# A fused layernorm, attention and FP4 feed-forward kernel: the feed-forward's inner values are kept in a pair of PSUM banks through SiLU's product and the quantizer

## The chip, the cores and the metric

The kernel runs on one core of one Trainium2 chip. The metric is the device time of one execution in microseconds (us). The kernel before takes 1505.81 us, the median of three runs (1504.54 to 1507.39).

## The reference, cut to what matters

The input `x` has the shape 4 x 2048 x 256, float32. The reference is a chain of four residual steps. Each one adds to `x` a function of `_layernorm(x)`: first attention a, then a feed-forward (FFN), then attention b, then the same FFN with the same weights.

```
def fp4_quant_dequant(x):                      # blocks of 16 along the last dimension
    scale = max(|block|) / 6, at least 1e-12
    q = nearest of {0, .5, 1, 1.5, 2, 3, 4, 6} to |block / scale|, with its sign, times scale
def fp4_linear(x, w): return einsum(fp4_quant_dequant(x), fp4_quant_dequant(w))
def ffn(x, w_gate, w_up, w_down):              # 256 -> 704 -> 256
    h = silu(fp4_linear(x, w_gate)) * fp4_linear(x, w_up)
    return fp4_linear(h, w_down)
```

Attention a normalizes its queries and keys over the whole tensor, and its output reduces to the value projection times s/s, so it needs one first pass over all of `x` (a Gram matrix). Attention b mixes the four rows of the leading dimension for each of the 2048 positions, in 16 heads of 16.

## The kernel before, in words

**Tiling.** The 2048 positions are cut into 16 groups of 128. A group is 128 partitions by 4 rows by 256 columns, so each of the two FFNs has 4 tiles of 128 rows in each group: 16 groups x 2 x 4 = 128 FFN tiles in all. The function `first_pass` prepares the weights and the Gram matrix; `group(j)` records everything that is done for one group.

**An FFN tile** (`ffn_tile`) goes over all five engines. TensorE multiplies the turned, quantized input with the gate and up weights, in two halves of 352 columns; each half has a PSUM bank for gate and one for up (line 1443). ScalarE takes SiLU of the gate half (L1464), and VectorE multiplies it with the up half and writes the product `h` to SBUF (L1475). The quantizer `to_grid` then works on all 704 columns of `h`, in SBUF: VectorE takes the block maxima and their reciprocals (`to_scales`, L383 and L384) and scales the values (`over_scales`, L388), ScalarE takes magnitudes (`to_steps`, L394), and VectorE rounds in two passes (`to_sum` L401, `from_sum` L404). The last pass writes bf16 values into `qm`. A DMA turns these (`gT`), other DMAs spread the turned scales (`hqT`, L1299), GpSimd multiplies the two (L1510), and TensorE multiplies with the down weights (L1547). The layout of `h` has a 17th column in each block that holds a constant floor for the scale, so L383 reads 748 columns.

**Other stages.** `attention_a` (projection at L1173 with `wvz`), `attention_b` (L1173 with `wqkB`, `wvgB`, `woB`; VectorE products at L1654 and sums at L1661, L1780, L1783; GpSimd at L1762), `ffn_in` (normalization and quantizer of the FFN's input, 1024 columns in one go), and `turn`, which transposes on TensorE (L1150) and drains on ScalarE (L1157).

**The order of the work.** Nothing is ordered by loops. Every step is recorded with `plan.op(engine, us, rank, fn, reads, writes, port)`: its engine, a cost in us, and a rank. `Plan.order` then plays the steps through by those costs. Whenever an engine is free, it takes the ready step of lowest rank whose buffers are free, and the instructions are emitted in the order in which the steps start. The engines' queues keep that order on the chip; semaphores make them wait for what isn't ready. The ranks come from the table `BEGIN`, with one row for each group.

**Two resources in the plan.** A step with `port=True` on VectorE or GpSimd takes a lock that the other's steps must wait for: the plan never lets two such steps overlap. All three quantizer passes of an FFN tile have `port=True` in the kernel before. Buffers come from pools: four PSUM banks called `mm` for gate and up halves, four called `bank` for everything else, three `h`, three `qa`, two `qm`, two `gT`, three `hqT`.

The costs that the plan uses are lines like these; 0.86 us is its price of one quantizer pass over 704 columns:

```
    SYNC = 0.08
    AHEAD = {"DVE": 0.15, "POOL": 0.08}
...
                {"amax": 1.32, "pass": 0.86, "abs": 0.74, "n": FF},
```

Of the kernel before, what the change touches and what calls it, by code (L numbers as in the profile page):

```python
# [18 lines left out]
P = 128  # L19
D = 256  # L20
# [4 lines left out]
HF = FF // 2  # L25
FB = FF // BLK

# [11 lines left out]
def blocks(ap, n=BLK):  # L39
    return ap.rearrange("p (g e) -> p g e", e=n)  # L40
# [17 lines left out]
class Plan:  # L58
# [4 lines left out]
    SYNC = 0.08  # L63

    WINDOW = 3.4133
    AHEAD = {"DVE": 0.15, "POOL": 0.08}
# [47 lines left out]
    def order(self, seed):  # L114
# [58 lines left out]
        while left:  # L173
            moved = False
            for e, ready in waiting.items():
# [42 lines left out]
                heapq.heappush(done, (now + us + o["land"], i))  # L218
# [5 lines left out]
            times = [t for t in free_at.values() if t > now + 1e-9]  # L224
# [8 lines left out]
            while done and done[0][0] <= now + 1e-9:  # L233
                t, i = heapq.heappop(done)
                for b in ops[i]["bufs"]:
                    b.left -= 1
                    if not b.left:
                        pools[b.pool].append(b.ap)
# [11 lines left out]
def kernel(  # L250
# [43 lines left out]
    banks = [one([P, 512], f"bank{i}", ps) for i in range(8)]  # L294
# [121 lines left out]
    plan.pool("mm", banks[:4])  # L416
    plan.pool("bank", banks[4:])
# [4 lines left out]
    floored += tiles("h", 3, [P, FB, BLK + 1], fp)  # L422
# [3 lines left out]
    tiles("sil", 2, [P, HF], fp)  # L426
    tiles("qa", 3, [P, FF], fp)

    for t in tiles("qm", 2, [P, 6 * P], fp, BF16):
        nc.gpsimd.memset(t[:, FF:], 0.0)  # L430
    tiles("gT", 2, [P, 6, P], fp, BF16)
# [3 lines left out]
    for t in tiles("hqT", 3, [P, 6, P], fp):  # L435
        nc.gpsimd.memset(t[P // 2 :, 5, :], 0.0)
# [15 lines left out]
    def first_pass():  # L452
        op = plan.op
        GRAM = [plan.given("bank", 2) for _ in range(KC)]
        gram = [b.ap for b in GRAM]

# [97 lines left out]
        def normalized_products(n, j):  # L554
# [3 lines left out]
            for s in range(S):  # L558
                op(
                    "ACT",  # L560
                    0.6,
# [89 lines left out]
        for ns in together:  # L651
            for n in ns:
# [21 lines left out]
                for s in range(S):  # L674
                    op(
                        "DVE",
                        0.465,
# [13 lines left out]
            if n >= SOON:  # L691
                op("POOL", 4.4, at + 3.0, lambda cut=cut: roots_later(cut), seen, done)
            else:
                y, _, v = (norm_tiles["a"][:, cut, i, :] for i in range(2, 5))
                op("DVE", 0.8, at + 0.5, lambda cut=cut: variances(cut), seen, done)
                op(
                    "ACT",
                    0.25,
# [6 lines left out]
                op("DVE", 1.0, at - 30.0, lambda cut=cut: inverses(cut), (), done)  # L705
# [11 lines left out]
        def quantize(at, load, p, n):  # L717
# [7 lines left out]
            def sc(i):  # L725
# [13 lines left out]
                0.25,  # L739
# [1142 lines left out]
```

## Time and profile before

| | |
|---|---|
| median of three runs | 1505.81 us (1504.54 to 1507.39) |
| the profiled execution: its time, its span | 1509.01 us, 1507.2 us |
| mean granted TensorE clock | 0.992 |
| PE (TensorE) busy | 1448.9 us, 96% of the span, 5742 matmul instructions |
| DVE (VectorE) busy | 1385.5 us, 92% |
| ACT (ScalarE) busy | 797.0 us, 53% |
| POOL (GpSimd) busy | 759.0 us, 50% |
| chain of work that ended last | PE 54%, DVE 22%, issue 4%, ACT 2%, POOL 1%, DMA 1% |

The profile page is of one execution. A row of its list of groups names a line of the kernel, the engine, the operation, what is written and read with shapes, and the count; then the busy time of all, the mean time of one, and the idle time of the engine just before them with what ended it. One float32 matmul of the program stands in the trace as two instructions. Matmuls overlap: the time of one contains the way through the array, so a matmul's mean time is longer than the distance at which matmuls follow each other. The table of waits sums, for each engine and line, the time that the engine stood idle and what released it. The timeline gives start, length, engine, line and count of instructions that follow each other.

### The profile page before, as it was taken

How to read it: one execution, taken by the hardware profiler on the slowest of the kernel's cores; microseconds unless marked ns; L12 is line 12 of the kernel's file. 1: busy time of each engine (PE TensorE's matmuls, PEld its weight loads, DVE VectorE, ACT ScalarE, POOL GpSimd, SP SyncE). 2: the span in 40 equal slices, each digit the busy share in tenths (PEclk: the TensorE clock that was granted, in tenths of full speed). 3: DMA queues.
4: the chain of work that ended last, by engine and by line, in shares of the span. 5: the costliest groups of instructions: out<-in, count | busy, mean ns of one | idle time of the engine just before them, and what ended most of it. 6: DMA issues, size and time to landing. Idle time of an engine off the chain costs nothing.

```text
span 1507.2 us, 19903 instructions
## 1 busy us (share of the span) xinstructions
PE 1448.9 (96%) x5742; PEld 1003.4 (67%) x5742; DVE 1385.5 (92%) x2139; ACT 797.0 (53%) x1696; POOL 759.0 (50%) x787
## 2 busy tenths in 40 slices
PE   7989999999999999999999999999979999999999
PEld 7746566666767676666666666677657766766676
DVE  7789899999999989999889999999989999899996
ACT  6556656542656355555375665365446543554342
POOL 5343455454754364544454654455655454754532
PEclk9999999999999999999999999999999999999999
DMA  9303321234432333233323332232323333322541
GB/s 280 91 1 51 61 35 19 46 60 79 88 61 50 63 65 70 62 67 64 67 47 60 67 57 59 50 61 61 59 42 65 63 58 67 65 47 49 95 80 42
DMA packets 220989, 96.86 MB, mean 64 GB/s; under 512 B 108240, under 2 KB 220624, under 8 KB 220880
## 3 DMA queue, kind: packets, MB, share of 16 engines
q1 hardware_dynamic: 220880, 95.60, 32.3%
q8 instruction: 45, 0.74, 0.2%
q14 instruction: 64, 0.52, 0.1%
HBM read 18.09 MB, written 8.39 MB: 18 GB/s over the span
## 4 chain that ended last, share of the span: by engine, by line
PE 54%; DVE 22%; issue 4%; ACT 2%; POOL 1%; DMA 1%; POOLq 0%; SPq 0%; DVEq 0%; ACTq 0%
PE bank L1443 24%; PE bank L1547 14%; PE bank L1173 12%; PE bank L1150 2%; DVE qa L401 2%; DVE sh L383 2%; DVE qa L388 2%; DVE qm L404 2%; DVE h L1475 2%; DVE pp L1654 2%; DVE pp L1780 2%; DVE sc L1661 1%; DVE x L335 1%; DVE qax L404 1%; DVE qax L401 1%
## 5 line engine op out<-in xcount | busy, mean ns | idle before, releaser
L1443 PE MATMUL bank<-wguT,turned 128*128 128x352 f32 x2048 | 641.1, 462 | 11.5 <-DVE h L1475 8.9
L1443 PEld LDWEIGHTS bank<-wguT,turned 128*128 128x128 f32 x2048 | 382.4, 191 | 219.2 <-issue 16.2
L1547 PE MATMUL bank<-wdT,hqT 128*128 128x256 f32 x1536 | 350.9, 380 | 4.4 <-POOL hqT L1510 3.1
L1510 POOL TENSOR_TENSOR hqT<-hqT,gT 128x768 f32<-128x768 f32 x124 | 231.1, 1869 | 214.1 <-DMA gT<-qm 68.9
L1547 PEld LDWEIGHTS bank<-wdT,hqT 128*128 128x128 f32 x1536 | 289.8, 190 | 63.8 <-POOL hqT L1510 8.5
L1464 ACT ACTIVATE sil<-bank 128x352 f32<-128x352 f32 x256 | 114.6, 454 | 114.6 <-PE bank L1443 88.4
L394 ACT ACTIVATE qm<-qa 128x704 bf16<-128x704 f32 (+2 forms) x136 | 105.6, 779 | 89.1 <-DVE qa L388 82.8
L1762 POOL TENSOR_TENSOR pp<-vg,sc 128x1024 f32<-128x1024 f32 x64 | 134.4, 2114 | 33.2 <-DVE tok L1783 28.8
L1475 DVE TENSOR_TENSOR h<-sil,bank 128x352 f32<-128x352 f32 x256 | 127.8, 506 | 24.9 <-ACT sil L1464 11.8
L401 DVE SCALAR_TENSOR_TENSOR qa<-qm,qa 128x704 f32<-128x704 bf16 (+2 forms) x136 | 137.9, 1014 | 12.9 <-ACT qm L394 12.8
L1266 POOL TENSOR_TENSOR qax<-qax,sx 128x1024 f32<-128x1024 f32 x32 | 71.1, 2222 | 127.9 <-DVE qax L404 95.8
L388 DVE SCALAR_TENSOR_TENSOR qa<-sh,h 128x704 f32<-128x704 f32 x128 | 131.6, 1038 | 0.7
L404 DVE SCALAR_TENSOR_TENSOR qm<-qm,qa 128x704 bf16<-128x704 bf16 x124 | 128.5, 1037 | 2.4
L1157 ACT COPY turned<-bank 128x512 f32<-128x512 f32 x160 | 87.5, 585 | 69.9 <-PE bank L1150 69.7
L1173 PE MATMUL bank<-wqkB,turned 128*128 128x512 f32 x256 | 123.3, 605 | 0.1
L383 DVE TENSOR_REDUCE sh<-h 128x44 f32<-128x748 f32 x128 | 119.1, 930 | 3.8
L1173 PE MATMUL bank<-wvz,turned 128*128 128x512 f32 x256 | 118.2, 595 | 2.1 <-ACT wdT L850 0.8
L341 ACT ACTIVATE dev<-x,norms_f 128x256 f32<-128x256 f32 x128 | 64.9, 507 | 56.0 <-DVE x L335 53.9
L1654 DVE TENSOR_TENSOR pp<-qk 128x1024 f32<-128x1024 f32 x64 | 84.4, 1319 | 0.4
L1173 PEld LDWEIGHTS bank<-wvz,turned 128*128 128x128 f32 x256 | 46.5, 190 | 49.1 <-issue 38.8
L377 ACT ACTIVATE xn<-x,norms_f 128x256 f32<-128x256 f32 x128 | 67.9, 592 | 20.6 <-POOL norms_f L371 16.8
L1661 DVE TENSOR_REDUCE sc<-pp 128x64 f32<-128x1024 f32 x64 | 77.6, 1213 | 1.3
(194 smaller groups left out, 2047.2 us busy)
## 6 DMA issues: line engine op xcount, KB each, us to landing
hqT<-sT SPq DMA_DIRECT2D x620, 64.0 KB
x<-in_L_attn_a_x_dram SPq DMA_DIRECT2D x23, 512.0 KB
out_dram<-x SPq DMA_DIRECT2D x64, 128.0 KB
hqT<-sT SPq DMA_DIRECT2D x124, 32.0 KB
gT<-qm SPq DMA_TRANSPOSE x124
hqT<-in_L_ffn_w_down_dram SPq DMA_DIRECT2D x2, 352.0 KB
hqT<-in_L_ffn_w_gate_dram SPq DMA_DIRECT2D x5, 128.0 KB
hqT<-in_L_ffn_w_up_dram SPq DMA_DIRECT2D x5, 128.0 KB
```

The source lines that it names most:

```text
L383: nc.vector.tensor_reduce(amax, src, AX.X, ALU.max, apply_absolute_value=True)
L388: nc.vector.scalar_tensor_tensor(blocks(a), over_blocks(rs), -6.0 * BELOW, src, ALU.mult, ALU.mult)
L401: nc.vector.scalar_tensor_tensor(a, m, FLOOR, a, ALU.max, ALU.add)
L404: nc.vector.scalar_tensor_tensor(a if to is None else to, m, FLOOR, a, ALU.max, ALU.subtract)
L1173: nc.tensor.matmul(bank.ap[:, :n], lhs.ap[:, c, s * P : (s + 1) * P], w[:, c, :], start=(c == 0), stop=(c == KC - 1),)
L1443: nc.tensor.matmul(bank.ap[:, :HF], xqT.ap[:, c, s * P : (s + 1) * P], w[:, c, cols], start=(c == 0), stop=(c == KC - 1),)
L1464: lambda g=g, sil=sil: nc.scalar.activation(sil.ap, g.ap[:, :HF], AF.Silu),
L1475: lambda u=u, sil=sil, half=half: nc.vector.tensor_mul(h.ap[:, half * FB // 2 : (half + 1) * FB // 2, :BLK], blocks(sil.ap), blocks(u.ap[: ...
L1510: lambda: nc.gpsimd.tensor_mul(hqT.ap, hqT.ap, gT.ap),
L1547: nc.tensor.matmul(o.ap[:, :D], hqT.ap[:, i, :], wdT[:, i, :], start=(i == 0), stop=(i == 5),)
L1654: nc.vector.tensor_mul(pr.ap, qk.ap[:, s : s + 1, :D].to_broadcast([P, S, D]), qk.ap[:, :, D:],)
L1762: nc.gpsimd.tensor_mul(pv.ap.rearrange("p t (n e) -> p t n e", e=HD), vg.ap[:, :, :D].rearrange("p t (n e) -> p t n e", e=HD), over_blocks ...
```

## The change

- **FFN tile.** The 704 columns are cut into 512 and 192 in place of 352 and 352. The first 512 gate columns go to a bank. The 512 up columns go to the first bank of a pair of banks (`pair`, two pairs in all); the remaining 192 up columns and the remaining 192 gate columns go to the second bank of the same pair (the step `rest`). The product with SiLU is written over the up values in the pair, the block maxima go into the pair's free columns, and the quantizer's passes work in place in the pair. Only the last pass writes to SBUF (`qm`). `h` and its 17th column are gone; the floor of the scale is a small extra VectorE instruction. The three passes no longer carry `port=True`.
- **Buffers.** Eight single banks become two pairs and four single banks; the pool `mm` is gone, so the gate bank comes from `bank` as all other products do. `qm` goes from 2 to 4, `gT` from 2 to 3, `hqT` from 3 to 4, `qa` from 3 to 2.
- **Plan.** A step's result now becomes available with a delay that depends on the engine that made it (`LATE`) and the one that takes it (`SYNC`); buffers come free with a delay; short GpSimd steps hold the lock for 0.1 us. Most costs are replaced by other figures, all in the same manner (0.43 to 0.336 and so on); `BEGIN` has new values throughout. With these, the whole order of instructions on every engine differs.

```diff
-    SYNC = 0.08
+    SYNC = {"POOL": 0.12}
+    LATE = {"PE": 0.163, "DVE": 0.08, "ACT": 0.097, "POOL": 0.04}
-    AHEAD = {"DVE": 0.15, "POOL": 0.08}
+    EARLY = {"DVE": 0.06, "POOL": 0.09}
...
-                    if holder != e and lock[other[e]] > now - 1e-9:
-                        us -= self.AHEAD[e]
-                        free_at[e] = now + us
-                    lock[e] = now + us
+                    small = e == "POOL" and us < 0.35
+                    lock[e] = now + (0.1 if small else us - self.EARLY[e])
...
-                    same = ops[n]["engine"] == ops[i]["engine"]
-                    ops[n]["at"] = max(ops[n]["at"], t + (0.0 if same else self.SYNC))
+                    f = ops[n]["engine"]
+                    late = 0.0 if f == e else self.LATE.get(e, 0.0) + self.SYNC.get(f, 0.035)
+                    ops[n]["at"] = max(ops[n]["at"], t + late)
...
-    banks = [one([P, 512], f"bank{i}", ps) for i in range(8)]
+    pairs = [one([P, 2, 512], f"pair{i}", ps) for i in range(2)]
+    banks = [one([P, 512], f"bank{i}", ps) for i in range(4)]
...
+            g, u, qm, sh = (plan.buf(p) for p in ("bank", "pair", "qm", "sh"))
+            def rest():
+                product(flat(HA, FF), wuT, HA, FF)
+                product(flat(FF, GE), wgT, HA, FF)
+            op("PE", 1.707, at, lambda: product(g.ap[:, :HA], wgT, 0, HA), x_w, [(g, 0)])
+            op("PE", 1.707, at + 1.7, lambda: product(flat(0, HA), wuT, 0, HA), x_w, [(u, 0)])
+            op("PE", 1.28, at + 3.4, rest, x_w, [(u, 1), (u, "gate")])
...
+                    lambda half=half, n0=n0, n1=n1: nc.vector.tensor_mul(
+                        flat(n0, n1), sil[half].ap, flat(n0, n1)
+                    ),
...
+            def hidden_scales():
+                nc.vector.tensor_reduce(
+                    flat(GE, GE + FB), blocks(flat()), AX.X, ALU.max, apply_absolute_value=True
+                )
+                nc.vector.tensor_scalar(
+                    sh.ap[:, 0, :], flat(GE, GE + FB), 6e-12, 0.0, ALU.max, ALU.add
+                )
+                nc.vector.reciprocal(sh.ap[:, 2, :], sh.ap[:, 0, :])
...
+            op("DVE", 1.5, at + 6, hidden_scales, HU, [(sh, 0)])
+            op("DVE", 0.81, at + 7, hidden_over_scales, [(sh, 0)], HU)
+            op("ACT", 0.68, at + 8, hidden_steps, HU, [(qm, 0)])
+            op("DVE", 0.81, at + 10, hidden_sum, [(qm, 0)], HU)
+            op("DVE", 0.81, at + 10.1, hidden_grid, HU + ([] if apart else [(qm, 0)]),
+               [(qm if apart else qa, 0)])
```

In the text below, a tile's "first product" is VectorE's product over the 512 columns, its "second product" that over the 192, and "second SiLU" is ScalarE's over the 192.

More of the change, by code (lines that the diff above doesn't have):

```diff
@@ L24 @@
 FF = 704
-HF = FF // 2
+HA = 512
 FB = FF // BLK
+GE = FF + FF - HA
 HC = [i * 128 for i in range(6)]
@@ L222, in order @@
                 continue
-            times = [t for t in free_at.values() if t > now + 1e-9]
+            times = [t for t in (*free_at.values(), *lock.values()) if t > now + 1e-9]
             times += [
@@ L414, in tiles @@
         return made
-    plan.pool("mm", banks[:4])
-    plan.pool("bank", banks[4:])
+    plan.pool("pair", pairs)
+    plan.pool("bank", banks)
     plan.pool("x", xs_of)
@@ L453, in first_pass @@
         op = plan.op
-        GRAM = [plan.given("bank", 2) for _ in range(KC)]
-        gram = [b.ap for b in GRAM]
+        GRAM = [plan.given("pair", 1)]
+        gram = [GRAM[0].ap[:, c] for c in range(KC)]
         XN = [plan.given(p, 0) for p in ("vg", "vg", "vz", "qk")]
@@ L891, in fold @@
         def fold(at, dst, token, lhs):
-            mm = plan.buf("mm")
+            mm = plan.buf("bank")
             def pe():
@@ L922, in center @@
         def center(at, w, n, tokens, bias=None):
-            mm = plan.buf("mm")
+            mm = plan.buf("bank")
             def pe():
@@ L1041, in first_pass @@
             op(
-                "DVE", 0.95, FIRST, square, [(mm, 0), (WQK, 0)], [(PROD, c), ("part", 2 + c)]
+                "DVE", 0.714, FIRST, square, [(mm, 0), (WQK, 0)], [(PROD, c), ("part", 2 + c)]
             )
-        tot = plan.buf("mm")
+        tot = plan.buf("bank")
         def total():
@@ new lines, in ffn_tile, with flat, product @@
+            sil = [plan.buf("sil"), plan.buf("silB")]
+            qa = None if apart else plan.buf("qa")
+            def flat(n0=0, n1=FF):
+                return u.ap.rearrange("p t n -> p (t n)")[:, n0:n1]
+            def product(to, w, n0, n1):
+                for c in range(KC):
+                    nc.tensor.matmul(
+                        to,
+                        xqT.ap[:, c, s * P : (s + 1) * P],
+                        w[:, c, n0:n1],
+                        start=(c == 0),
+                        stop=(c == KC - 1),
+                    )
```

261 lines of the change are left out of this document (128 added, 133 removed).

## The prediction

> **What bounds the kernel now.** First the page: which engines are full, and whose work the chain of waits that ended last is made of.
>
> ```profile
> PE 1448.9 (96%) x5742; PEld 1003.4 (67%) x5742; DVE 1385.5 (92%) x2139; ACT 797.0 (53%) x1696; POOL 759.0 (50%) x787
> ...
> PE 54%; DVE 22%; issue 4%; ACT 2%; POOL 1%; DMA 1%; POOLq 0%; SPq 0%; DVEq 0%; ACTq 0%
> ```
>
> TensorE and VectorE are both nearly full, and the chain changes between them. How much of "96%" is work? A matmul's length contains its way through the array, so I take the distance between matmuls from a stretch of the timeline in which TensorE never stands still.
>
> ```profile
> 708.38 2.53 PE L1443 MATMUL bank<-wguT,turned 128*128 128x352 f32 x8
> ...
> 710.75 0.27 PE L1282 MATMUL bank<-ident,sh 128*44 128x128 f32 x1
> ...
> 710.86 1.88 PE L1173 MATMUL bank<-wvz,turned 128*128 128x512 f32 x4
> ...
> 712.58 1.04 PE L1150 MATMUL bank<-ident,x 128*128 128x128 f32 x8
> ```
>
> Start to start: eight of 352 columns take 2.37 us (0.296 each), one of 128 takes 0.11, four of 512 take 1.72 (0.430 each). The time is proportional to the columns, so 256 cost 0.216, 288 cost 0.242. With the counts of the list of groups: 2048 x 0.296 = 606, 1536 x 0.216 = 332 (down), 512 x 0.430 = 220, 256 x 0.242 = 62, 256 x 0.216 = 55, 764 transposes x 0.11 = 84, the Gram matrix 128 x (0.216 + 0.11) = 42, weights about 15: **1416 us of pure matmul work**. The span is 1507, so 91 us are TensorE's loss, some 11 of them before the first and after the last matmul and **80 us in stalls**. The table of waits of TensorE says behind whom:
>
> ```profile
> PE bank L1443 <- DVE h L1475: 8.9, 6, 4.4
> PE bank L577 <- ACT vg L377: 7.7, 1, 7.7
> PE bank L1150 <- DVE tok L1783: 6.6, 5, 2.1
> PE bank L1282 <- DVE sh L383: 4.4, 5, 1.2
> PE bank L1150 <- DVE vz L1325: 3.6, 1, 3.6
> PE bank L1150 <- POOL qax L1266: 3.5, 6, 1.4
> ```
>
> Mostly VectorE, or GpSimd, which itself waits for VectorE. So VectorE's delays are what a change could win back, and 80 us is the ceiling. Now VectorE's instructions line by line (shortest/median/longest in ns):
>
> ```profile
> L388 DVE SCALAR_TENSOR_TENSOR qa<-sh,h x128: 827/883/3034, 122.4 to 1491.2; 128x704 f32<-128x704 f32 x128
> L404 DVE SCALAR_TENSOR_TENSOR qm<-qm,qa x124: 828/891/2503, 127.4 to 1469.6; 128x704 bf16<-128x704 bf16 x124
> L1475 DVE TENSOR_TENSOR h<-sil,bank x256: 460/511/524, 118.5 to 1489.2; 128x352 f32<-128x352 f32 x128
> L335 DVE SCALAR_TENSOR_TENSOR x<-bank,x x128: 360/416/426, 138.9 to 1447.1; 128x256 f32<-128x256 f32 x128
> L335 DVE SCALAR_TENSOR_TENSOR x<-vz,x x64: 410/418/1945, 88.1 to 1179.7; 128x256 f32<-128x256 f32 x64
> ```
>
> The median is the undisturbed time. Instructions with two inputs in SBUF are sometimes two to four times as long; those with an input in a bank never are, not once in 384. The timeline shows what the long ones wait for:
>
> ```profile
> 720.91 0.88 DVE L388 SCALAR_TENSOR_TENSOR qa<-sh,h 128x704 f32<-128x704 f32 x1
> ...
> 723.39 1.64 POOL L1510 TENSOR_TENSOR hqT<-hqT,gT 128x768 f32<-128x768 f32 x1 [4.50 <-DMA gT<-qm]
> ...
> 723.69 2.09 DVE L388 SCALAR_TENSOR_TENSOR qa<-sh,h 128x704 f32<-128x704 f32 x1
> ```
>
> The second L388 starts inside a GpSimd product that runs to 725.03, and takes 1.2 us more than the first. That is the lock that `port=True` stands for; the plan avoids it, the chip still meets it.
>
> **The change, part by part.**
>
> *TensorE's products.* Per tile, before: 16 x 0.296 = 4.74 us. After: 8 of 512 and 8 of 192 columns (midway between 128 and 256: 0.163), 3.44 + 1.30 = 4.74. No difference; a weight load of 190 ns in front of a matmul of 0.163 us is no new limit, as the transposes follow each other at 0.11 with loads of 141 to 146.
>
> *The three passes leave the lock.* Mean less median on the page: L388 1038 - 883 = 155 ns x 128, L401 1031 - 884 = 147 x 130, L404 1037 - 891 = 146 x 124: **-57 us of VectorE's time**. Each pass has one SBUF input after the change, like the L335 with `bank`, which never waits. The other SBUF pairs (L1780 950 against 683 ns x 64, L1783 625 against 424 x 64, L335 with `vz`, L1654, the 1024-column passes) lose another 60 us to the lock. GpSimd has as much to do as before but meets half as many VectorE instructions that want the lock: undisturbed, the passes are 382 x 0.80 = 306 us (0.80: distance from 720.91 to the next VectorE start, 721.71), the others, by the same reckoning from their columns, 270. The waits that stay may fall as far as by half or not at all, since a new order shuffles them: 0 to -60, I take **-30**.
>
> *Speed of the passes in a pair.* L335 at 256 columns takes 416 ns with an input in a bank and 418 without: reading a bank costs nothing here. The Trainium skill speaks against this edit (VectorE: DVE Perf Modes, The TRN2 errata): it gives 120 cycles of fixed cost with a PSUM source against 58 from SBUF; as an estimate, five instructions per tile would pay 65 ns each, 41 us in all, and the gain below would shrink by some 20 us. A VectorE write into a bank stands nowhere in the trace. Bounds from L1475, which reads a bank: it varies from 460 to 524 ns about 511, so -50 to +15 ns, and as a read might hide what a write doesn't I allow +50; four large writes per tile make -26 to +26 us. I take 0, as all rows at hand are alike on both sides.
>
> *Scales.* Before: maxima 0.930 and reciprocal 0.428. After: 704 columns in place of 748 (0.88 in proportion), the floor as an instruction that the reciprocal waits for (L1715, with 128 columns, 0.217), the same reciprocal: +0.16 us per tile, **+20 us**.
>
> *SiLU and products.* Two of 352 against 512 + 192: the same columns, the same count. ScalarE stands idle 47% of the span and hides any difference.
>
> *Waits that the order adds.* In the changed program's order, the first product stands behind `rest` in 97 of 128 tiles and waits for it, although it needs only the other bank: both write the tile `pair`. In 57 of these the second SiLU in turn waits for the first product. On VectorE everything else queues behind the first product: passes, reductions, drains of other groups, and GpSimd and TensorE behind those. `rest` lasts 8 x 0.163 = 1.3 us, so the price is 0 (VectorE came late anyway) to 57 x 1.3 = 74 us; VectorE is over 90% taken and comes late often: **+18**. In 12 tiles nothing lies between the two products: SiLU (0.3) and two handovers, about 0.4 each, +5. In 25 tiles `rest` is emitted later and waits for the first product, on TensorE itself: at most 0.6 us each, 0 to 15 us, I take **5 us of TensorE**.
>
> *Two pairs.* Before, TensorE got its banks back after L1475. Now the up product waits for the last quantizer pass of two tiles earlier; 77 of 128 carry that wait explicitly. From the end of the up product to the last pass the chain is at least 1.3 (`rest`) + 0.3 + 0.35 (second product) + 0.88 + 0.22 + 0.43 + 0.88 + 0.79 + 0.88 + 0.89 = 6.9 us and eight handovers, with 0.1 to 0.2 each some 8 us. TensorE's own work between the end of an up product and the next one into the same pair, added up along the new order: 16.7 us in the median, under 9 in 11 of 126 cases. So tightness is rare: about 11 x 0.5 = **5 us** on TensorE; bounds 0 and 77 x 1 us.
>
> *The rest.* SBUF buffers (`qm`, `gT`, `hqT`) grow: ScalarE's 5 us behind `gT` go, hidden. DMAs and GpSimd's instructions are the same in number. Costs in the plan buy nothing themselves; the ones before are up to a third off the trace (0.43 us for L335, which lies 0.34 before its successor in the timeline), those after are near it.
>
> *Sum.* VectorE: -57 - 30 + 20 + 23 = **-44 us**. What is this worth? If only by VectorE's share of the chain, 22%, 10 us; if VectorE were the sole bound, 44. Both engines are nearly full and TensorE's stalls are mostly behind VectorE, so I take 0.7: -31. TensorE's new waits give back 10: **-21 us**. The profiled execution, 1509 us, would be 1488; the median of runs lies 3.2 us under it, so 1505.8 - 21 is about **1485 us**.
>
> **Rivals.**
> - *The lock was holding the whole plan.* Its exclusions also forced idle time on both engines that no row calls contention: the passes (306) + the others (270) + POOL (759) = 1335 us of 1507 had to go one after another; without the passes it is about 1030. Then the new order halves TensorE's 80 us of stalls: 1466, and 1455 if two thirds go. For it: VectorE's 122 us of idle time at 92% load. Against it: the order can't see the `pair` waits.
> - *Two pairs are too few (slower).* VectorE runs behind the plan, each late pass holds a pair, and TensorE stops. The 77 marked products decide: the gain of 21 is used up at 0.27 us more per product; at 0.6 us the time is 1505.8 - 21 + 46 - 5 = 1526. For it: there is no `h` any more for TensorE to run ahead into, and VectorE is still made late by GpSimd at times that the plan doesn't foresee (1.9 us at the longest for L335 with `vz`, 2.9 for L1780). Against it: the median of 16.7 us between reuses.
> - *It comes to nothing.* VectorE's relief is spent in waiting for `rest` at the upper price, 74: the sum is about +12 us on VectorE, TensorE's stalls stay: 1503 to 1515.
>
> **How the numbers follow.** Forecast 1475 to 1498 with chance 0.46; the lock held the plan 0.26; two pairs 0.17; nothing 0.11. Faster by over 0.2% (3 us, about what a measurement can tell from no change): 0.46 + 0.26 = 0.72; same 0.07, from the last case; slower 0.04 of that case and 0.17 = 0.21. The range for 8 in 10 goes from 1455, the low end of the first rival, to 1512, in the lower part of the second.
>
> **What would show it.** Right: the passes at 0.88 us in mean as in median; VectorE under 1340 us busy; TensorE's matmul work the same and its stalls near 60 us; a few us of waits of the FFN's products behind the last pass. Wrong: passes longer than 0.95 us undisturbed (writes into banks cost), or the up product waiting over 25 us in all behind the last pass (two pairs), or VectorE idle behind `rest` for over 40 us.

## The result and the profile after

The changed kernel takes **1545.6 us** (median of four runs, 1544.4 to 1547.6), the kernel before 1505.2 us on the same chip: a ratio of 1.0268, 95% interval 1.0251 to 1.0286. It is 40 us slower, where 21 us faster was forecast. The profiled execution has a span of 1543.1 us at a mean granted clock of 0.997 (0.992 before).

The page after, busy times and the chain that ended last:

```profile
PE 1458.3 (95%) x5742; PEld 968.8 (63%) x5742; DVE 1352.0 (88%) x2267; ACT 796.1 (52%) x1696; POOL 681.4 (44%) x787
...
DVE 43%; PE 39%; issue 5%; ACT 5%; POOL 4%; DMA 3%; SPq 0%; POOLq 0%; ACTq 0%; DVEq 0%
```

VectorE is busy for 33.5 us less than before (1385.5), and yet the chain runs through it for 43% of the span instead of 22%. TensorE's matmul work is still 1416 us by the prediction's reckoning (the same columns and the same count). The span less this work and the same 11 us of edges leaves 1543.1 - 1416 - 11 = 116 us of stalls, where before had 80 and the forecast 60.

The passes in the list of groups (line, engine, operation, shapes, count; busy us, mean ns; idle before), three rows of before and three of after:

```profile
L401 DVE SCALAR_TENSOR_TENSOR qa<-qm,qa 128x704 f32<-128x704 bf16 x130 | 134.1, 1031 | 12.8 <-ACT qm L394 12.8
L388 DVE SCALAR_TENSOR_TENSOR qa<-sh,h 128x704 f32<-128x704 f32 x128 | 131.6, 1038 | 0.7
L404 DVE SCALAR_TENSOR_TENSOR qm<-qm,qa 128x704 bf16<-128x704 bf16 x124 | 128.5, 1037 | 2.4
```

```profile
L394 DVE SCALAR_TENSOR_TENSOR pair<-sh,pair 128x704 f32<-128x704 f32 x128 | 114.2, 892 | 2.9
L407 DVE SCALAR_TENSOR_TENSOR pair<-qm,pair 128x704 f32<-128x704 bf16 x128 | 113.8, 889 | 15.6 <-ACT qm L400 15.3
L410 DVE SCALAR_TENSOR_TENSOR qm<-qm,pair 128x704 bf16<-128x704 bf16 x124 | 109.8, 885 | 3.5
```

The means are now what the medians were (883 to 891): the lock is gone from the passes, and in these rows reading and writing a pair costs at most 9 ns (892 against 883). So this part of the change did what it was to do, and the kernel is slower. The table of waits (engine, tile and line, releaser: us in all, times, longest), two rows of before and five of after:

```profile
POOL hqT L1510 <- DMA gT<-qm: 68.9, 19, 11.8
POOL hqT L1510 <- DMA hqT<-sT: 38.9, 7, 13.9
```

```profile
POOL hqT L1545 <- DMA gT<-qm: 198.8, 43, 11.0
POOL hqT L1545 <- DMA hqT<-sT: 135.8, 23, 20.9
DVE pair L1486 <- PE pair L1449: 33.6, 33, 4.1
DVE pair L1486 <- ACT silB L1475: 20.7, 27, 2.4
PE pair L1449 <- DVE qm L410: 13.8, 17, 1.8
```

GpSimd waits for DMAs for 335 us ahead of its `hqT` product, before 108. That is the loudest row, and the runs below speak against it as the cause. VectorE's products wait 54 us in all for TensorE's products into the pair and for the second SiLU (only a part of this is owed to the shared tile, see e1); TensorE's up product waits 13.8 us behind the last pass.

How one of the 17 comes about, in the timeline (start, length):

```profile
761.89 5.72 POOL L1797 TENSOR_TENSOR pp<-vg,sc 128x1024 f32<-128x1024 f32 x3
...
766.36 1.80 DVE L1815 TENSOR_TENSOR pp<-pp 128x512 f32<-128x512 f32 x1
...
770.14 0.87 DVE L407 SCALAR_TENSOR_TENSOR pair<-qm,pair 128x704 f32<-128x704 bf16 x1
...
771.04 0.89 DVE L410 SCALAR_TENSOR_TENSOR qm<-qm,pair 128x704 bf16<-128x704 bf16 x1
...
772.08 2.12 PE L1449 MATMUL pair<-wguT,turned 128*128 128x512 f32 x5 [1.80 <-DVE qm L410]
```

L1815 (0.68 us when undisturbed) meets a row of GpSimd products and takes 1.80, 1.1 us more. Everything behind it in VectorE's queue comes later: ScalarE had its magnitudes ready at 767.5, L407 starts at 770.14, and TensorE stands for 1.80 us because the pair is not free. The plan keeps such products apart by its figures; on the chip they met. By these lengths some 1.1 of the 1.80 us are owed to that; the rest of the queue in front of L407 is the plan's own order.

### The profile page after: what moved, and what is told of

Same layout as the page of the kernel before. It is cut to its first block, busy times and chain, and to the rows that moved or that the text cites. A ratio compares the mean times of both kernels' runs of the same rounds, so it can differ in the third digit from the quotient of the medians.

```text
span 1543.1 us, 20005 instructions
## 1 busy us (share of the span) xinstructions
PE 1458.3 (95%) x5742; PEld 968.8 (63%) x5742; DVE 1352.0 (88%) x2267; ACT 796.1 (52%) x1696; POOL 681.4 (44%) x787
## 4 chain that ended last, share of the span: by engine, by line
DVE 43%; PE 39%; issue 5%; ACT 5%; POOL 4%; DMA 3%; SPq 0%; POOLq 0%; ACTq 0%; DVEq 0%
PE pair L1449 11%; PE bank L1582 9%; PE bank L1179 9%; DVE pair L1486 5%; PE bank L1449 4%; DVE pair L1496 4%; DVE pair L407 3%; DVE qm L410 3%; DVE pair L394 3%; DVE pp L1689 3%; DVE sc L1696 3%; DVE x L341 2%; PE pair L583 2%; DMA gT<-qm 2%; DVE sh L1502 2%
## 5 line engine op out<-in xcount | busy, mean ns | idle before, releaser
L1449 PE MATMUL pair<-wguT,turned 128*128 128x192 f32 (+1 forms) x1536 | 420.8, 418 | 23.1 <-DVE qm L410 13.8
L1545 POOL TENSOR_TENSOR hqT<-hqT,gT 128x768 f32<-128x768 f32 x124 | 216.4, 1746 | 404.2 <-DMA gT<-qm 198.8
L1449 PEld LDWEIGHTS pair<-wguT,turned 128*128 128x128 f32 x1536 | 261.1, 190 | 169.6 <-issue 117.8
L1449 PE MATMUL bank<-wguT,turned 128*128 128x512 f32 x512 | 237.8, 594 | 2.4 <-DVE x L341 2.3
L400 ACT ACTIVATE qm<-pair 128x704 bf16<-128x704 f32 x128 | 96.7, 755 | 184.7 <-DVE pair L394 182.9
L1449 PEld LDWEIGHTS bank<-wguT,turned 128*128 128x128 f32 x512 | 93.3, 190 | 86.9 <-issue 75.3
L1797 POOL TENSOR_TENSOR pp<-vg,sc 128x1024 f32<-128x1024 f32 x64 | 129.4, 2039 | 33.5 <-DVE tok L1818 29.9
L1486 DVE TENSOR_TENSOR pair<-sil,pair 128x512 f32<-128x512 f32 x128 | 88.4, 692 | 48.3 <-PE pair L1449 33.6
L407 DVE SCALAR_TENSOR_TENSOR pair<-qm,pair 128x704 f32<-128x704 bf16 x128 | 113.8, 889 | 15.6 <-ACT qm L400 15.3
L1496 DVE TENSOR_REDUCE pair<-pair 128x44 f32<-128x704 f32 x128 | 115.1, 899 | 4.1
L394 DVE SCALAR_TENSOR_TENSOR pair<-sh,pair 128x704 f32<-128x704 f32 x128 | 114.2, 892 | 2.9
L410 DVE SCALAR_TENSOR_TENSOR qm<-qm,pair 128x704 bf16<-128x704 bf16 x124 | 109.8, 885 | 3.5
```

What stands on the lines that cost most here:

```text
L394: nc.vector.scalar_tensor_tensor(blocks(a), over_blocks(rs), -6.0 * BELOW, src, ALU.mult, ALU.mult)
L407: nc.vector.scalar_tensor_tensor(a, m, FLOOR, a, ALU.max, ALU.add)
L410: nc.vector.scalar_tensor_tensor(a if to is None else to, m, FLOOR, a, ALU.max, ALU.subtract)
L1449: nc.tensor.matmul(to, xqT.ap[:, c, s * P : (s + 1) * P], w[:, c, n0:n1], start=(c == 0), stop=(c == KC - 1),)
L1486: lambda half=half, n0=n0, n1=n1: nc.vector.tensor_mul(flat(n0, n1), sil[half].ap, flat(n0, n1)),
L1496: nc.vector.tensor_reduce(flat(GE, GE + FB), blocks(flat()), AX.X, ALU.max, apply_absolute_value=True)
```

## The experiments

**A measure for the reading.** The kernel computes, when it is built, where its plan ends by its own cost figures (`self.end` in `Plan.order`, the start of the last step). The chip's time less this end is called the **lag** here: what the chip needs and the plan didn't know. It is a difference of a measured number and a number of the kernel, no property of the chip. The ends come from the ranks too; several tables that had to be found anew end later than the old one, so kernels with different tables are compared by the lag as well as by the time. The lag is not fixed by the figures alone: e2 has all the new ones and a lag of 57, with an end 55 us later than e3's.

| run | data path | figures and rules of the plan | plan's end | time, us | lag |
|---|---|---|---|---|---|
| before | SBUF | old | 1470 | 1505.8 | 36 |
| e8, e9 | SBUF | old, ranks varied | 1471, 1473 | 1514.2, 1513.2 | 43, 40 |
| e11, e12 | SBUF | old, ranks found afresh | 1494, 1495 | 1523.9, 1532.2 | 30, 37 |
| e13 | SBUF | SyncE's figures new | 1493 | 1526.8 | 34 |
| e14 | SBUF | rules new | 1510 | 1534.3 | 24 |
| e7 | SBUF | VectorE's figures new | 1464 | 1537.1 | **74** |
| e3 | SBUF | all new | 1449 | 1531.0 | **82** |
| e2 | SBUF | all new, ranks of before | 1504 | 1560.9 | 57 |
| e15 | pair | old, plan told of the waits in the pair | 1504 | 1537.8 | 34 |
| e5 | pair | old | 1475 | 1533.7 | 59 |
| e6 | pair, gate's last columns apart | old | 1475 | 1522.1 | 47 |
| e16 | pair | old, VectorE's for the pair's steps without slack | 1494 | 1591.0 | **97** |
| e1 | pair, gate's last columns apart | new | 1443 | 1532.5 | 90 |
| e4 | pair, up in one go, plan told | new | 1467 | 1548.1 | 81 |
| after | pair | new | 1443 | 1545.6 | **103** |
| e10 | pair | new, ranks varied | 1445 | 1556.4 | 112 |

**First round: is it the pair or the plan?** Three theories stood: W, waits between steps that only share a pair; P, two pairs are too few; O, the new order and plan themselves.

e1_same_order keeps the changed kernel's order and takes the wait out of the data: where a single bank is empty at that point (105 of 128 tiles), the last gate columns go there, and the last up columns come directly behind the first 512.

```diff
 def rest():
-    product(flat(HA, FF), wuT, HA, FF)
-    product(flat(FF, GE), wgT, HA, FF)
+    if "ap" not in own:
+        product(flat(HA, FF), wuT, HA, FF)
+    product(gates[1](), wgT, HA, FF)    # own["ap"][:, :192] if "ap" in own else flat(FF, GE)
```

> The changed kernel with its own order of steps, but in the 105 tiles of 128 where a bank stands empty at that place the last 192 gate columns go to that bank in place of the pair, and the last 192 up columns are multiplied directly behind the first 512. So the pair has no second writer or reader while the first product runs; nothing else moves. Theory W (waits between steps that only share the tile pair, which the plan's costs leave out, made the 40 us): most of the loss goes, 1495 to 1515 us, and the first product waits for TensorE far less than the 33.6 us after. Theory P (two pairs are too few, TensorE is held behind the last pass): 1535 to 1550, no change. Theory O (the new order itself is worse): 1535 to 1550.

1532.5 us, ratio 1.0177 (1.0160 to 1.0193), between the range of W and that of P and O: in the same order of steps, 13 us of the 40 are waits of this kind. The first product's wait for TensorE did not fall far: 26.9 us are left of the 33.6, and 14.4 of the 20.7 behind the second SiLU. So 13 of the 54 us went; the rest stays, though 105 tiles no longer share.

e2_sbuf_old_ranks is the changed kernel's plan (rules, delays, figures) with before's tile (SBUF `h`, 352 columns, lock on the passes) and before's ranks; e3_sbuf_new_ranks is the same with ranks searched for that plan.

```diff
-    SYNC = 0.08
+    SYNC = {"POOL": 0.12}
+    LATE = {"PE": 0.163, "DVE": 0.08, "ACT": 0.097, "POOL": 0.04}
...
-                {"amax": 1.32, "pass": 0.86, "abs": 0.74, "n": FF},
+                {"amax": 1.28, "pass": 0.802, "abs": 0.69, "n": FF},
```

> The plan's part of the change alone: LATE, SYNC, EARLY, the short GpSimd locks and all costs as in the changed kernel, but the feed-forward's inner values in SBUF as before (352 + 352 columns, h, eight single banks), and the ranks of before. Theory W and theory P: the plan is no cause of loss, 1490 to 1515. Theory O (costs and delays as traced make a worse order): 1525 or more.

> As e2, with ranks searched anew for it against the plan's own end, as the changed kernel has ranks of its own. Theory W: with inner values in SBUF the plan knows every wait, and new ranks pay: 1460 to 1490, faster than both kernels. Theory O: an order drawn so tightly breaks on the chip whatever holds the values, 1520 to 1550.

1560.9 us (1.0361, 1.0342 to 1.0381) and 1531.0 us (1.0169, 1.0141 to 1.0196). The new plan makes the old tile slower, by 25 us even with ranks searched for it (e3). Theory O holds for a large part.

e4_free gives the last gate columns a bank of their own in every tile, puts all 704 up columns first and lets the plan know it, with ranks searched for it.

```diff
-    g, u, qm, sh = (plan.buf(p) for p in ("bank", "pair", "qm", "sh"))
+    g, gB, u, qm, sh = (plan.buf(p) for p in ("bank", "bank", "pair", "qm", "sh"))
```

> The pair kept, without the shared-tile waits in any tile, and the plan told so: all 704 up columns go to the pair first, the last 192 gate columns to a bank of their own; ranks searched anew for it, since those of the changed kernel leave the plan without a step that can go on. Two pairs and four banks as in the changed kernel. Theory W: 1480 to 1505. Theory P: the pairs are as few, 1530 or more. Theory O: 1530 or more.

1548.1 us (1.0286, 1.0264 to 1.0308), no better than the change: with a bank less for everything else, its plan ends 24 us later. In this one table, the bank cost as much as the waits that it took away.

**Second round: the tile under the old plan, and one engine's figures.** e5_pair_old_plan has the pair, with the old rules and figures; e6_pair_old_plan_apart adds e1's edit to the very same order; e7_old_plan_new_dve is before with only VectorE's figures new.

```diff
 e5:  op("DVE", 0.86, at + 7, hidden_over_scales, [(sh, 0)], HU)     # after: 0.81
 e7: -  {"amax": 1.32, "pass": 0.86, "abs": 0.74, "n": FF},
     +  {"amax": 1.28, "pass": 0.802, "abs": 0.74, "n": FF},
     -  0.43,     # L1567
     +  0.279,
```

> The tile's part of the change alone (PSUM pair, 512 and 192 columns, its buffers), under the rules and the cost figures of the plan before; the new steps get figures with the same slack as the old ones (a pass 0.86 us, the scales 1.65, the products 0.66 and 0.33), the ranks were searched anew. VectorE's figures then sum to 1370 us. They sum to 1309 us in the kernel before, whose VectorE was busy 1385.5 us, to 1256 in the changed kernel (busy 1352.0) and to 1225 in the two runs with the plan's part alone (busy 1381.1 and 1393.8). Theory F (the plan's new figures are too short, so that it puts instructions into the queues closer than the chip can do them): most of the loss goes, 1480 to 1510 us, and GpSimd's wait of the hqT product for gT falls from 198.8 us to about 100. Theory T (the pair itself costs the time: two pairs, steps that wait for the whole pair): 1525 to 1550. Theory R (any ranks found by a search on the plan alone are worse on the chip than the table of the kernel before): 1520 to 1545.

> The same order as in e5_pair_old_plan, but as in e1_same_order the last 192 gate columns go to a bank that is empty then, where there is one, and the last 192 up columns follow directly on the first 512. Under the changed kernel's plan this edit took 13 us. Theory F and theory T both expect that a good part of it is there again: 5 to 15 us less than e5_pair_old_plan; if the waits inside the pair only filled time that the order had lost anyway, the difference is under 4 us.

> The kernel before with its data path, its rules of the plan and its figures for SyncE, TensorE, ScalarE and GpSimd; only VectorE's figures are those of the changed kernel's plan (a pass 0.802 for 0.86, maxima and reciprocals 1.28 for 1.32, sums 0.279 for 0.43 and so on; their sum falls from 1309 to 1225 us, the chip's VectorE needs 1385), and the ranks were searched anew. Theory F, with VectorE as the engine whose figures matter: slower than before by 20 to 55 us (1525 to 1560). If it is SyncE's figures or the rules of handover that matter: within 12 us of before. Theory R: slower than before by 15 to 40, as everything with ranks of the search.

1533.7 us (1.0194, 1.0174 to 1.0213), 1522.1 us (1.0105, 1.0078 to 1.0133) and 1537.1 us (1.0226, 1.0195 to 1.0256). Theory F was too hopeful for e5: with figures that are no longer short the pair is still 29 us slower than before, inside the ranges of T and R, and 12 of the 29 are the waits that e6 takes away in the same order. e7, with the figures of one engine changed and ranks searched for them, is 32 us slower, inside the ranges of F and R; what part the new ranks have in it is the question of the third round.

**Third round: or is any new order slow?** All these tables of ranks were new. e8 and e9 vary before's table at random, e10 the changed kernel's; e11 and e12 have tables from an unrelated start. Nothing else is changed.

```diff
-        (-975, -236, -544, -316, -60, -261),
+        (other ranks, 16 rows)
```

> The kernel before with nothing changed but its table of ranks: the ranks were varied at random as long as the plan, by its own figures, ended within 3 us of where it ends with the old table. 58% of the pairs of neighbours in TensorE's queue and 52% of those in VectorE's stay as they were. Theory R (the old table holds an order that was good on the chip for reasons that the plan's figures don't know, and any other order that the plan thinks as good loses time): 1520 to 1540 us, near e5_pair_old_plan (1533.7) and e3_sbuf_new_ranks (1531.0). Theories F (too short figures) and T (the pair): the figures and the data path are those of before, so 1500 to 1512.

> The same with another random course: 64% of the pairs of neighbours in TensorE's queue stay, 61% in VectorE's. Theory R: 1515 to 1540. Theories F and T: 1500 to 1512. The distance between this run and e8_before_other_ranks shows how far two orders that the plan holds equal lie apart on the chip.

> The changed kernel with nothing changed but its table of ranks, varied in the same way (ends within 3 us of the old table by the plan's figures); 42% of the pairs of neighbours in TensorE's queue stay. If the changed kernel's table is as good as any that its plan would call equal: 1535 to 1555. If it was a lucky or an unlucky one, over 12 us away from 1545.6; theory R says unlucky or neutral, not lucky, since nothing of its order has the old table's advantage.

> The kernel before, its figures and its data path, with ranks that a search found from an unrelated table, so that 32% of the neighbours in TensorE's queue and 27% of those in VectorE's are as before (e8_before_other_ranks: 58% and 52%). The kernel computes when it is built where its plan ends by its own figures (self.end in Plan.order); what the chip needs beyond that is called the lag here. Ends and lags so far: before 1470 and 36 us, e8 1471 and 43, e9 1473 and 41, with the old figures and old data path; e7 (only VectorE's figures new) 1464 and 73; e3 (all figures and rules new) 1449 and 82; e2 1504 and 57; the pair under the old figures, e5, 1475 and 59, e6 1475 and 47; the changed kernel 1443 and 102, e10 1445 and 112. This table ends at 1494. Theory F (the lag comes from the figures): the figures are those of before, so a lag of 36 to 50, 1530 to 1544 us. Theory R (the lag is low only near the old table, whose order was good on the chip for other reasons): a lag of 60 to 80, 1554 to 1574 us.

> The same with a second table, of another ancestry (29% of the neighbours in TensorE's queue and 25% in VectorE's as in before, 33% and 29% as in e11_before_fresh_ranks); its plan ends at 1495 us. Theory F: a lag of 36 to 50, 1531 to 1545 us. Theory R: 60 to 80, 1555 to 1575 us.

e8 1514.2 us (1.0041, 1.0019 to 1.0063), e9 1513.2 (1.0051, 1.0034 to 1.0068), e10 1556.4 (1.0343, 1.0316 to 1.0369), e11 1523.9 (1.0119, 1.0104 to 1.0134), e12 1532.2 (1.0180, 1.0159 to 1.0201). e8 and e9 lie just above the range of F and T and under that of R, e10 1 us above its range, e11's lag under both of its ranges. Both tables of the two kernels were some 8 to 11 us better than other tables with the same end, so that part of theory R is true, but it is alike on both sides and doesn't explain the 40. The lag of the fresh tables, 30 and 37, is that of before: with the old figures it doesn't grow when the order is new, and theory R as it was put for these two runs (a lag of 60 to 80) falls. In time it does not: every table searched for the old tile, whatever its figures, lies between 1524 and 1537 us (e3, e7, e11 to e14), inside the 1520 to 1545 that R gave for e5, and e7 is only some 5 and 13 us slower than e12 and e11, 23 and 24 slower than e8 and e9. The difference is that the plan foretold the slow tables of e11 and e12, which end 24 us late by its figures, and did not foretell that of e7.

The pages of e11 (old figures) and e7 (VectorE's new), in this order:

```profile
PE 1456.4 (96%) x5742; PEld 1005.2 (66%) x5742; DVE 1391.6 (91%) x2139; ACT 796.7 (52%) x1695; POOL 750.9 (49%) x787
```

```profile
PE 1454.4 (95%) x5742; PEld 1003.2 (65%) x5742; DVE 1397.6 (91%) x2139; ACT 794.7 (52%) x1694; POOL 755.0 (49%) x787
```

The same work on every engine. What differs is what the plan believes of it: VectorE's figures, summed over all steps of the kernel, give 1309 us in e11 and 1225 in e7.

A plan can be played with other figures in a given order; this needs the kernels alone, no run. With VectorE's new figures the orders of before, e8, e9, e11 and e12 end within 3 us of where they end with the old ones. e7's order ends at 1464 by the new figures and at 1513 by the old. So VectorE's shorter figures add no lag to an order that was found with the old ones; the lag belongs to the order that a search finds with the new ones. The old figures would have put that order 43 us behind that of before, and the chip puts it 32 behind.

**Fourth round: which of the new figures, and what of the pair.** e13_old_plan_new_sync has only SyncE's figures new, e14_old_plan_new_rules only the rules.

```diff
 e13: -  op("SP", 4.9, at + 1, spread, [(sT, 0)], [(dst, "scale")], land=3.3)
      +  op("SP", 4.9, at + 1, spread, [(sT, 0)], [(dst, "scale")], land=2.7)
 e14: -  ops[n]["at"] = max(ops[n]["at"], t + (0.0 if same else self.SYNC))
      +  late = 0.0 if f == e else self.LATE.get(e, 0.0) + self.SYNC.get(f, 0.035)
      +  ops[n]["at"] = max(ops[n]["at"], t + late)
```

> The kernel before with only SyncE's figures as in the changed kernel: the spread of the scales lands after 2.7 us (before 3.3), the transposing DMA takes 1.4 + 1.75 us (before 2.0 + 2.5), the output lands after 2.0 (before 4.0); ranks searched anew, the plan ends at 1493 us by its figures. The changed kernel's GpSimd waited 334.6 us for these two DMAs ahead of its hqT product, that of before 107.8. If VectorE's figures make the lag and SyncE's don't: a lag of 30 to 45 as in the five runs with the old figures, 1523 to 1538 us. If SyncE's figures make it too: a lag of 55 to 80, 1548 to 1573 us, and GpSimd's wait for gT well over 110 us.

> The kernel before, all figures and the data path as they were, with the new rules of the plan (a result is available with a delay by the engines on both sides, 0.075 to 0.283 us for the flat 0.08; buffers come free later; the lock is held differently); ranks searched anew, the plan ends at 1510 us by its figures. The new rules are the more cautious ones at every handover between engines, so if the figures make the lag it is 20 to 40 here: 1530 to 1550 us. If the rules themselves cost time, the lag is over 55: 1565 us or more.

1526.8 us (1.0154, 1.0135 to 1.0174) and 1534.3 us (1.0197, 1.0180 to 1.0214): lags of 34 and 24. Neither makes it; that the more cautious rules give a smaller lag than before's 36 is about the scatter of orders. And e13's waits show what GpSimd's waiting is worth:

```profile
POOL hqT L1510 <- DMA gT<-qm: 191.3, 41, 12.5
POOL hqT L1510 <- DMA hqT<-sT: 83.2, 13, 16.6
```

Nearly the 198.8 us of the changed kernel behind `gT`, at a lag like that of before; e7, with a lag of 74, has 103.8 and 48.1 in these rows. The wait and the lag don't go together.

e15_pair_old_plan_told is e5 with a plan that knows that the steps of a pair wait for each other; e16_pair_tight_dve is e5 with VectorE's figures for the pair's steps without slack (and two small ones of other engines lowered with them: TensorE's 1.73 for a product to 1.717, ScalarE's 0.74 for the magnitudes to 0.68).

```diff
 e15: -  op("PE", 1.3, at + 3.4, rest, x_w, [(u, 1), (u, "gate")])
      +  op("PE", 1.3, at + 3.4, rest, x_w, [(u, 0), (u, 1), (u, "gate")])
      -  [(u, half)] + ([(u, "gate")] if half else []),
      +  [(u, half), (u, "gate")],
 e16: -  op("DVE", 0.86, at + 7, hidden_over_scales, [(sh, 0)], HU)
      +  op("DVE", 0.8, at + 7, hidden_over_scales, [(sh, 0)], HU)
```

> As e5_pair_old_plan (pair, old rules, old figures with slack), but the plan is told that the products into the pair and the step called rest wait for each other, as they do on the chip because they write one tile; ranks searched anew for it, and the plan ends at 1504 us by its own figures (e5: 1475). If these untold waits are the pair's part of the lag: a lag of 24 to 43 as without the pair, 1528 to 1547 us. If the pair lags for another reason: 50 to 65, 1554 to 1569 us.

> As e5_pair_old_plan, but with figures without slack for the pair's own steps on VectorE (passes 0.80, 0.86, 0.80 for three times 0.86, scales 1.60 for 1.65, products 0.60 and 0.33 for 0.66 and 0.33): VectorE's figures sum to 1342 us instead of 1370, and the plan, ranks searched anew, ends at 1494 us. If the missing slack adds to the lag here as it did without the pair (84 us less in the sum gave 30 to 43 us more): a lag of 65 to 75, 1559 to 1569 us. If in the pair VectorE's figures don't matter: 50 to 62, 1544 to 1556 us.

1537.8 us (1.0210, 1.0182 to 1.0237), a lag of 34 as without the pair, and 1591.0 us (1.0561, 1.0531 to 1.0591), a lag of 97. The first row is e5's wait of VectorE's products for TensorE, the second e15's:

```profile
DVE pair L1482 <- PE pair L1445: 49.0, 45, 4.4
```

```profile
DVE pair L1482 <- PE pair L1445: 27.1, 25, 4.4
```

Told of the waits, the plan places other work in front of them; the lag falls by 25 us, though its plan also ends 29 us later, so nothing is won in time. Two tables are compared here; played in their own orders with these waits counted, e5's plan ends at 1511 instead of 1475 and the changed kernel's at 1472 instead of 1443, so 36 and 29 us of their lags are waits that the plan left out. For e16 the expectation was too small: 28 us less in the figures gave 38 us more lag.

**The sum.** The change's plan ends 27 us earlier (1470 to 1443) and its lag is 67 us larger (36 to 103); the difference is the 40. From single steps: VectorE's figures 31 to 43 (e7 against e8, e9, e11 and e12), the untold waits in the pair 25 (e5 against e15): 36 + 56 to 68 = 92 to 104 us of lag. Orders with equal figures differ by up to 10 us in lag either way, so the two shares are known to about that much. e3's 82 leaves room for some 10 us more from the other new figures (TensorE's sum to 1417 instead of 1431).

A part of the 67 us only moves the yardstick: by all the new figures and rules, before's own order ends at 1457. With this one yardstick the changed kernel's order, its waits in the pair counted, ends at 1472. That is 15 us of the 40; the other 25 are lag on top of it, 74 against 49. The runs agree in size: 13 us by e1 in the same order, 25 us by e3 without the pair.

No version beat the kernel before; the best with the pair was e6, 1.0% slower.

## Why the prediction was wrong

**Right.** The passes leave the lock: -57 forecast; the means less the old means, 146 x 128 + 142 x 128 + 152 x 124 ns, make -56. The passes in a pair at their old speed: they are (885 to 892 ns). The text's aside on the other case, five instructions at 65 ns each, would have taken 0.7 x 41 = 29 us of the gain by its own rate, not some 20. The Trainium skill's rule that spoke against the edit (VectorE: DVE Perf Modes, The TRN2 errata: 120 cycles with a PSUM source against 58) is not what these rows show, and the decision to follow L335's rows was right. The scales, +20: 899 + 203 + 428 ns against 930 + 428 make +22. TensorE's products of 192 columns, midway at 0.163 us:

```profile
767.10 1.46 PE L1449 MATMUL pair<-wguT,turned 128*128 128x192 f32 x8
...
768.40 1.88 PE L1449 MATMUL bank<-wguT,turned 128*128 128x512 f32 x4
```

1.30 us for eight, 0.163 each. Other lock waits, -30 with a range of 0 to -60: over the length that a quarter of each group stays under, VectorE's instructions lost 124 us before and 47 after, so 77 in all and 21 beside the passes. Two pairs, 5 us on TensorE: 13.8 measured, nearly three times the term, but under the 25 that the text set as its limit for that rival. Two of the text's own signs were not met: VectorE is busy for 1352.0 us and not under 1340, and TensorE's stalls are 116 us and not near 60.

**Wrong, first: "Costs in the plan buy nothing themselves."** The text saw that the new figures lay near the trace and the old ones "up to a third off", and took this for a change without effect. The third was slack, and the step that failed is to have put this term at nothing. VectorE's figures sum to 1309 us before and its instructions kept it busy for 1385.5, 77 more; with the new figures the old tile has 1225 against 1397.6 (e7), 173 more; the changed kernel 1256 against 1352.0, 96 more. The plan puts VectorE's instructions, and everything that hangs on them, closer than the chip does them, and the search then picks an order that is early only by these figures. e7 prices VectorE's part at 31 to 43 us of lag, of which 5 to 24 are seen in time against other tables with the old figures; e3 prices the whole new plan, with its table, at 25 us in time. It should have been a term of the sum, on the side of the loss.

Where do figures "near the trace" fall short? They are the distance between two instructions that have nothing to do with each other. From VectorE's timeline of the changed kernel:

```profile
708.67 0.90 DVE L407 SCALAR_TENSOR_TENSOR pair<-qm,pair 128x704 f32<-128x704 bf16 x1 [0.17 <-ACT qm L400]
709.60 0.89 DVE L410 SCALAR_TENSOR_TENSOR qm<-qm,pair 128x704 bf16<-128x704 bf16 x1
710.40 0.75 DVE L1331 SCALAR_TENSOR_TENSOR vz<-bank,norms_a,bvz 128x512 f32<-128x512 f32 x1
```

L1331 starts 0.80 us after L410 and needs nothing of it; L410 starts 0.93 us after L407, whose result it reads. The figure for both passes is 0.81. These are no single cases: over all places without idle time L407 is followed after 0.92 us in the median by a step that needs its result (103 places) and after 0.80 by one that doesn't (23). In the whole timeline, over all places where a VectorE instruction follows another without idle time, the distances exceed the figures by 104 us in the changed kernel, 65 of them in the 446 places where the second instruction reads what the first wrote; the other 39 are of the size of the lock's share (47 us lost after the change, see above). In the kernel before it is 79 us, 39 of them in 322 such places: its slack, 0.86 (for two of the three passes) and 0.44 for distances of 0.80 and 0.43, covered much of this. In e7 it is 174 us, 63 of them in 349 such places. The lag doesn't follow this sum one to one (lags of 36, 103 and 74), so the sum shows that the figures are short, not how much each place costs.

**Wrong, second: the rate of 0.7.** VectorE's relief was forecast as -67 us of work and +23 of waits. Its busy time fell by 33.5 us (the lengths sum to 45 less, but more of them now stand one behind the other's result), and its idle time rose from 122 to 191 us. None of the relief became time, and a smaller rate would not have mended the sum. With the pair, the old figures and the waits told (e15), the lag is 34, that of before, with VectorE busy 1367.0 against 1385.5. As these runs read, the stalls of TensorE are made less by how much VectorE has to do than by how far it comes behind the place that the plan gave it; a plan with less work for VectorE packs it as tightly as its figures allow. No run shows this by itself.

**Wrong, third: the shared tile.** The waits of the first product were priced at +18 + 5 on VectorE (0 to 74) and 5 on TensorE. The table has them at 33.6 and 20.7 us of VectorE's idle time, inside the bounds, and the text's limit of 40 for the row behind `rest` was not passed. But priced by what removing them brings in the same order, they are 12 to 13 us (e1, e6), and by what the plan leaves out, 25 us of lag (e15) or 29 (the changed kernel's order played with them). The text, by its rate of 0.7, counted 21, between these. The mechanism was right; some 8 us of size were off.

The forecast's chances were made of cases that all took the plan's figures for harmless. Its slower rival, two pairs too few (1526), named another mechanism: the 17 waits behind the last pass are real, but they are one of the places where the lag shows, as the timeline above has it, and a pair in the old plan with the waits told has no more lag than SBUF.

**What stays open.** Why 28 us less in VectorE's figures gave 38 us more lag in e16 (its mean granted clock, 0.981 against 0.994 in e5, may have a part in it), and which steps of VectorE's figures weigh most: each run is one order, and orders with the same figures scatter by 10 us. On the old tile, no run has a table searched anew with the old figures that ends as early as before's, so how much of the 25 us any searched table would have cost stays open too. Whether the pair with figures that count the result of the instruction before (0.93 instead of 0.81) and told waits would beat the kernel before was not settled: even the table found for e15 ends 34 us later than the old one's, and that difference alone makes up e15's distance to the kernel before.

## What to carry to other kernels

Where a plan with cost figures makes the order, the figures are part of the kernel: correcting them towards the trace can take away slack that covered lock waits, handovers and results that the next instruction needs, and it has to be priced like any edit. When engines are freed and nothing comes of it, compare how far the chip lags behind the plan, not how much work is left. And tell the planner every wait that a shared tile brings, or the end that it computes can't be believed: in the changed kernel 29 us were missing.

## What was not expected of the hardware

VectorE's distance between instructions depends on whether the second needs the first: 0.80 us against 0.93 us for the same 704-column pass (medians of 0.26 against 0.40 for the product of 192 columns). The Trainium skill (VectorE: DVE Perf Modes, The DRAIN you can't avoid) says that the next operation does not start until the pipe is empty, and adds that one that is not held starts earlier. The row of L1331 is a case of the second: it doesn't need L410's result and starts 0.09 us before L410's end in the trace. Writes into a pair of PSUM banks, 704 columns across the border of two banks, cost hardly more than writes into SBUF (892 ns mean against a median of 883 for the same pass).
